# Attention values weighed in four column tiles of 32 instead of two of 64

## The chip, the cores and the metric

The kernel runs on one core of a Trainium2 chip. The metric is the device time of one execution in microseconds (us). The engines are named as the profile names them: PE is TensorE's matmuls and PEld its weight loads, DVE is VectorE, ACT is ScalarE, POOL is GpSimd, SP is SyncE.

## The reference, cut to what matters

64 graphs of 256 nodes with 512 features go through two layers of masked attention, each with a residual. All is float32.

```python
# layer 0: 4 heads of 64
h = relu(layernorm(x)); q, k, v = h @ Wq, h @ Wk, h @ Wv
sim = where(adj, einsum('bhid,bhjd->bhij', q, k) * 64**-0.5, -max)
x = x + einsum('bhij,bhjd->bhid', softmax(sim), v) @ Wo + bo
# layer 1: 8 heads of 64, the diagonal always allowed
h = relu(layernorm(x)); h = layernorm(h) * gamma + beta
q, k, v = split(h @ w_qkv.T, 3)
scores = where(adj | eye, einsum('bihd,bjhd->bhij', q, k) * 64**-0.5, -1e9)
x = x + einsum('bhij,bjhd->bihd', softmax(scores), v) @ w_out.T + b_out
```

The line that the change touches is the weighing of values, `softmax(sim) @ v`.

## The kernel before, in words

The kernel works in 32 steps of two graphs (`G` is 2, `g` counts them). Layer 0 of a step has 2 pairs of heads and layer 1 has 4, so a step has 6 units, a unit being one pair of heads (`pr`; `e` is the head in the pair) for both graphs: 192 units in all. Features or keys lie on the 128 partitions.

A unit goes through these functions:

- `scores` (L770): keys on partitions, queries along the free dimension. A head has 64 features, so the two heads use the two row halves of the array: 8 matmuls (2 graphs, 2 halves of the 256 keys, 2 heads) of 256 columns, into four PSUM tiles `sc`.
- `mask_scores` (L783, DVE) adds the mask, `exponentials` (L788, ACT) gives `p`, and `key_halves` (L792, POOL) adds the two key halves into `pd`.
- `weigh` (L802): the product of v and `p` over the 256 keys, into one PSUM tile `po` whose partitions are the 128 features of the pair. The weights that stay in the array are 128 keys by 64 features of v, so two heads stand side by side in the two column halves of the array. ACT copies `po` out (L816). Then come the sums over keys (L822): a block of 32 columns of ones times `pd`, four matmuls, one for each graph and head, in the four column quarters of the array. DVE takes reciprocals (L827) and their maximum (L828), and SP spreads them with eight DMAs.
- `normalise` (L843, POOL) multiplies by the reciprocals.

Around these stand the projections, as seven products of half-size blocks: `project_qk` (L679; L621, L625 and L627 are among its evacuations by DVE, and L689 is a multiplication on POOL that layer 0's q needs), `project_v0` (L706), `project_v1` (L720), the output products `combine0` (L731) and `combine1` (L745), and the transposes `transpose_h` (L600).

The order is written out by hand. Every call gets a due time in periods of 6.13 places (`at`, `at_dense`, `visit`), the calls are sorted by it, and each engine takes its instructions in that order; nothing reorders them afterwards. A `visit` puts one unit's `weigh` directly before the next unit's `scores`, so PE's stages follow as projection, weighing (L802), sums (L822), scores (L770), projection. PSUM is split into four tiles for scores and weighing (`ps_sc`) and four banks used in turn for all else (`mm_tile`).

Of the kernel before, what the change touches and what calls it, by code (L numbers as in the profile page):

```python
# [315 lines left out]
def fast_path(  # L316
# [20 lines left out]
    P = 128  # L337
    B, N, D = x.shape
    DH = 64
    G = 2  # L340
    NSTEP = B // G
    NIC = N // P
# [20 lines left out]
    def mm_tile(shape, dt=FP, hold=False):  # L363
        tag = next(b for b in banks if b not in held)
        banks.remove(tag)
        banks.append(tag)
        if hold:
            held.add(tag)
        return ps_mm.tile(shape, dt, name="mm", tag=tag)
# [424 lines left out]
    def weigh(s, lyr, pr, first):  # L794
        st = S[s]
        p, pd = st.pop(("p", lyr, pr))
        po = ps_sc.tile([P, G, N], FP, name="sc")
        for g in range(G):
            for kc in range(NIC):
                for e in range(2):  # L800
                    c0 = pr * P + e * DH
                    nc.tensor.matmul(  # L802
                        po[e * DH:(e + 1) * DH, g, :],
                        st[f"v{lyr}"][:, g * NIC + kc, c0:c0 + DH],
                        p[e][:, g, kc, :], start=(kc == 0), stop=(kc == NIC - 1),
                    )
        if lyr == 0:
            if first:
                st["oT0"] = act.tile([P, PR0, G, N], FP, name="oT0")
            dst = st["oT0"][:, pr]  # L810
        else:
            if first:
                st["oT1"] = act.tile([P, NB + 1, HP1, N], FP, name="oT1")
            b0, b1, step = B_OF[pr // HP1]
            dst = st["oT1"][:, b0:b1:step, pr % HP1, :]
        nc.scalar.copy(dst, po)  # L816

        sums = mm_tile([P, N])
        for g in range(G):
            for e in range(2):  # L820
                r0 = 32 * (2 * g + e)
                nc.tensor.matmul(  # L822
                    sums[r0:r0 + 32, :], ones, pd[:, e, g, :], start=True, stop=True
                )
        inv = sm.tile([P, N], FP, name="inv", bufs=1)
        for i in range(2):
            nc.vector.reciprocal(inv[:, i * P:(i + 1) * P], sums[:, i * P:(i + 1) * P])  # L827
        nc.vector.tensor_tensor_reduce(  # L828
            out=sums, in0=sums, in1=inv, scale=1.0, scalar=0.0, op0=ALU.add, op1=ALU.max,
            accum_out=extremes[:, units[0]:units[0] + 1],  # L830
        )
        units[0] += 1
        invb = sm.tile([P, G, N], FP, name="invb", bufs=1)
        for g in range(G):
            for e in range(2):
                r0 = 32 * (2 * g + e)
                for d0 in range(e * DH, (e + 1) * DH, 32):
                    nc.sync.dma_start(invb[d0:d0 + 32, g, :], inv[r0:r0 + 32, :])  # L838
        st["dst", lyr, pr] = dst, invb
# [29 lines left out]
    def visit(period, w, prev, cur):  # L869

        w -= 0.0003
        if 0 <= prev[0] < NSTEP:
            at(period, w, weigh, *prev)
            at(period, w + 0.55, normalise, *prev[:3])
        if 0 <= cur[0] < NSTEP:
            at(period, w, scores, *cur)
            at(period, w, mask_scores, *cur, 0)
            at(period, w + 0.05, exponentials, *cur, 0)
            at(period, w + 1 / 7, mask_scores, *cur, 1)
            at(period, w + 0.18, exponentials, *cur, 1)  # L880
            at(period, w + 0.2, key_halves, *cur, 0)
            at(period, w + 0.3, key_halves, *cur, 1)

    AT_C0, AT_Q0, AT_V0, AT_H1, AT_C1 = 3.0, 3.57, 4.57, 5.13, 5.131
    for s in range(-2, NSTEP):
        p = s
# [6 lines left out]
    for s in range(NSTEP):  # L893

        p = s - 2
# [14 lines left out]
        p = s - 1  # L910
# [13 lines left out]
        p = s  # L924
# [69 lines left out]
```

## Time and profile before

| what | value |
|---|---|
| time, median of 3 | 3520.03 us (3518.53 to 3522.54) |
| span of the profiled execution | 3519.7 us |
| PE busy | 3429.8 us, 97% |
| PEld, DVE, POOL, ACT busy | 75%, 57%, 54%, 35% |
| matmul records of the weighing, L802 | 3072 |
| matmul records of the sums over keys, L822 | 1536 |
| mean granted TensorE clock | 0.993 |

Busy time is a share of the span; an engine's idle time costs nothing unless another waits for it. A group such as `128*64 128x256 f32` is a matmul with 128 rows and 64 columns of the array in use, on a moving operand of 128 partitions by 256 float32. A float32 matmul leaves two records of matmul and two of weight load. The end of a matmul is modelled, so matmuls overlap in the record, and the distance between starts tells more than a duration.

### The profile page before, as it was taken

To read this page: it belongs to the slowest core of one execution; us is meant where nothing else is said; L and a number is where in the kernel's file an instruction comes from. 1 tells how busy PE (TensorE), PEld (TensorE's weight loads), DVE (VectorE), ACT (ScalarE), POOL (GpSimd) and SP (SyncE) were. 2 spreads that over 40 slices of the span, in tenths; PEclk is the share of its full clock that TensorE was granted. 3 is DMA by queue.
4 is the path that set the end of the run, shared out by engine and by line. 5 is a ranking of instruction groups with operands and counts; after the bars stand their busy time and mean duration, and the time that the engine had idled before them with its cause. 6 is when DMAs were issued, how large, how long until landed. Compare 5 with 4: busy or idle time off the path is not lost.

```text
span 3519.7 us, 52762 instructions
## 1 busy us (share of the span) xinstructions
PE 3429.8 (97%) x19555; PEld 2633.3 (75%) x19586; DVE 1988.8 (57%) x3681; ACT 1224.1 (35%) x2065; POOL 1905.5 (54%) x1643
## 2 busy tenths in 40 slices
PE   5999999999999999999999999999999999999997
PEld 3777777777777777777777777777777777777765
DVE  4465565555655555655655655556556556556553
ACT  2333333333333333333333333333333333333321
POOL 3556545556545565455565455665555654555642
PEclk9999999999999999999999999999999999999999
DMA  4011111110111111111111111101111111111011
GB/s 136 23 53 34 47 41 52 54 52 27 44 51 52 53 50 31 42 53 53 53 32 44 47 52 53 52 27 44 51 53 53 42 38 41 53 53 52 16 40 37
DMA packets 146968, 165.57 MB, mean 47 GB/s; under 512 B 43272, under 2 KB 94992, under 8 KB 146704
## 3 DMA queue, kind: packets, MB, share of 16 engines
q1 hardware_dynamic: 141312, 155.30, 14.8%
q10 hardware_dynamic: 5392, 6.82, 0.6%
q8 instruction: 157, 2.57, 0.3%
q14 instruction: 107, 0.88, 0.1%
HBM read 78.12 MB, written 33.55 MB: 32 GB/s over the span
## 4 chain that ended last, share of the span: by engine, by line
PE 88%; DVE 6%; POOL 2%; SPq 1%; DMA 1%; issue 1%; ACT 0%; ACTq 0%; POOLq 0%; DVEq 0%
PE mm L679 27%; PE mm L720 11%; PE mm L745 11%; PE sc L770 10%; PE sc L802 10%; PE mm L706 6%; PE mm L731 6%; PE mm L600 3%; PE mm L822 3%; SPq L838 1%; DVE bs L536 1%; DVE p L783 1%; POOL xt L493 1%; DVE ve L588 1%; DVE inv L827 1%
## 5 line engine op out<-in xcount | busy, mean ns | idle before, releaser
L792 POOL TENSOR_TENSOR pd<-p 128x512 f32<-128x512 f32 x384 | 485.8, 1280 | 1080.4 <-ACT p L788 1076.4
L679 PE MATMUL mm<-hT,wqkv 128*128 128x256 f32 x3584 | 802.0, 381 | 1.6
L679 PEld LDWEIGHTS mm<-hT,wqkv 128*128 128x128 f32 x3584 | 673.4, 190 | 111.4 <-issue 20.9
L788 ACT ACTIVATE p<-p 128x512 f32<-128x512 f32 x768 | 461.1, 629 | 509.9 <-DVE p L783 508.7
L827 DVE RECIPROCAL inv<-mm 128x128 f32<-128x128 f32 x384 | 339.5, 926 | 329.5 <-PE mm L822 309.0
L783 DVE TENSOR_TENSOR p<-sc,n 128x512 f32<-128x512 f32 x768 | 481.1, 682 | 2.2 <-PE sc L770 2.2
L816 ACT COPY oT<-sc 128x512 f32<-128x512 f32 x192 | 112.5, 586 | 1044.4 <-PE sc L802 1044.4
L679 PE MATMUL mm<-hT,wqk 128*128 128x256 f32 x1792 | 408.6, 383 | 11.9 <-DVE qk L621 11.8
L679 PEld LDWEIGHTS mm<-hT,wqk 128*128 128x128 f32 x1792 | 335.7, 190 | 90.7 <-DVE qk L621 23.8
L745 PE MATMUL mm<-wo,oT 128*128 128x256 f32 x1792 | 395.4, 381 | 5.9 <-POOL oT L843 5.9
L720 PE MATMUL mm<-wqkv,hT 128*128 128x256 f32 x1792 | 395.3, 381 | 0.0
L770 PE MATMUL sc<-qk 64*128 64x256 f32 x3072 | 386.6, 390 | 6.3 <-DVE qk L625 3.6
L802 PE MATMUL sc<-p,v 128*64 128x256 f32 x3072 | 379.4, 387 | 6.1 <-ACT p L788 6.1
L720 PEld LDWEIGHTS mm<-wqkv,hT 128*128 128x128 f32 x1792 | 337.8, 190 | 55.2 <-issue 10.6
L745 PEld LDWEIGHTS mm<-wo,oT 128*128 128x128 f32 x1792 | 339.7, 191 | 52.4 <-POOL oT L843 6.7
L770 PEld LDWEIGHTS sc<-qk 64*128 64x128 f32 x3072 | 280.1, 186 | 115.3 <-issue 65.8
L802 PEld LDWEIGHTS sc<-p,v 128*64 128x64 f32 x3072 | 205.9, 137 | 155.8 <-issue 61.9
L843 POOL TENSOR_TENSOR oT<-oT,invb 128x512 f32<-128x512 f32 x192 | 244.7, 1275 | 79.2 <-DMA invb<-inv 60.0
L648 POOL TENSOR_TENSOR xt<-xt,u 128x512 f32<-128x512 f32 x96 | 121.8, 1270 | 252.5 <-DVE xt L642 188.9
L550 ACT ACTIVATE h<-h,mr,r 128x512 f32<-128x512 f32 x256 | 203.3, 808 | 131.9 <-POOL mr L546 131.9
L638 DVE TENSOR_TENSOR xt<-mm,xt 128x512 f32<-128x512 f32 x64 | 44.3, 692 | 330.8 <-PE mm L745 330.8
L731 PE MATMUL mm<-wo,oT 128*128 128x512 f32 x512 | 230.6, 593 | 0.0
(104 smaller groups left out, 3821.4 us busy)
## 6 DMA issues: line engine op xcount, KB each, us to landing
invb<-inv SPq DMA_DIRECT2D x1536, 32.0 KB, 1.8
h<-in_x_dram SPq DMA_DIRECT2D x32, 1024.0 KB, 5.1
xt<-in_x_dram SPq DMA_DIRECT2D x32, 1024.0 KB, 5.1
out_dram<-xt SPq DMA_DIRECT2D x32, 1024.0 KB, 4.7
ad<-in_adj_dram SPq DMA_DIRECT2D x32, 128.0 KB, 4.4
wr<-in_L_gnn_w_qkv_dram ACTq DMA_DIRECT2D x3, 1024.0 KB, 10.3
wr<-in_L_gnn_w_out_dram ACTq DMA_DIRECT2D x1, 1024.0 KB, 14.4
wqk<-in_L_gnn_Wq_dram ACTq DMA_DIRECT2D x4, 128.0 KB, 5.1
```

The source lines that it names most:

```text
L679: nc.tensor.matmul(bank[:, k, :], w[:, wa, c, k, a * P:(a + 1) * P], st["hT"][:, ba, c, :], start=first and (k, c) == (0, 0), stop=(k, c) ...
L706: nc.tensor.matmul(bank, st["hT"][:, b0 + t // NIC * step, c % HC, i:i + P], wv0[:, c, :], start=(c == 0), stop=(c == NC - 1),)
L720: nc.tensor.matmul(bank[:, t, :], st["hT"][:, ba, c, t * P:(t + 1) * P], wqkv1[:, wa, c, 2, :], start=first and (t, c) == (0, 0), stop=(t, ...
L731: nc.tensor.matmul(bank, st["oT0"][:, pr, t // NIC, t % NIC * P:(t % NIC + 1) * P], wo0[:, pr, :], start=(pr == 0), stop=(pr == PR0 - 1),)
L745: nc.tensor.matmul(bank[:, t, :], st["oT1"][:, ba, c, t * P:(t + 1) * P], wo1[:, wa, c, :], start=first and (t, c) == (0, 0), stop=(t, c) ...
L770: nc.tensor.matmul(sc[g][e][:, kc, :], qk[rows, 1, k0:k0 + P], qk[rows, 0, g * N:(g + 1) * N], start=True, stop=True,)
L783: nc.vector.tensor_tensor(p[e][:, g], sc[e], neg[:, :, g, :], ALU.add)
L788: nc.scalar.activation(p[e][:, g], p[e][:, g], AF.Exp, scale=SCALE)
L792: nc.gpsimd.tensor_tensor(pd[:, e], p[e][:, :, 0, :], p[e][:, :, 1, :], ALU.add)
L802: nc.tensor.matmul(po[e * DH:(e + 1) * DH, g, :], st[f"v{lyr}"][:, g * NIC + kc, c0:c0 + DH], p[e][:, g, kc, :], start=(kc == 0), stop=(kc ...
L827: nc.vector.reciprocal(inv[:, i * P:(i + 1) * P], sums[:, i * P:(i + 1) * P])
L843: nc.gpsimd.tensor_tensor(dst, dst, invb, ALU.mult)
```

## The change

The weighing is cut finer: each head's 64 features of v become two blocks of 32, so that the array stands in four column tiles of 32, as it does for the sums over keys which follow. One head's two tiles read the same `p`. The purpose is that weighing and sums need no change of tiling between them. It is the only edit; the lines after it move up by one, so the weighing is L801 and the sums are L821 in the changed kernel.

```diff
         po = ps_sc.tile([P, G, N], FP, name="sc")
         for g in range(G):
             for kc in range(NIC):
-                for e in range(2):
-                    c0 = pr * P + e * DH
+                for r0 in range(0, P, 32):
                     nc.tensor.matmul(
-                        po[e * DH:(e + 1) * DH, g, :],
-                        st[f"v{lyr}"][:, g * NIC + kc, c0:c0 + DH],
-                        p[e][:, g, kc, :], start=(kc == 0), stop=(kc == NIC - 1),
+                        po[r0:r0 + 32, g, :],
+                        st[f"v{lyr}"][:, g * NIC + kc, pr * P + r0:pr * P + r0 + 32],
+                        p[r0 // DH][:, g, kc, :], start=(kc == 0), stop=(kc == NIC - 1),
                     )
```

The number of matmuls in a unit's weighing goes from 8 to 16, each with half the columns and the same 256 moving columns. Semaphores and the order of everything else are as before.

## The prediction

> **What bounds the kernel now.** I read the page's busy shares and its chain that ended last, then the costliest groups, then the chain and the timeline of one short stretch.
>
> ```profile
> span 3519.7 us, 52762 instructions
> PE 3429.8 (97%) x19555; PEld 2633.3 (75%) x19586; DVE 1988.8 (57%) x3681; ACT 1224.1 (35%) x2065; POOL 1905.5 (54%) x1643
> ...
> PE 88%; DVE 6%; POOL 2%; SPq 1%; DMA 1%; issue 1%; ACT 0%; ACTq 0%; POOLq 0%; DVEq 0%
> ...
> L802 PE MATMUL sc<-p,v 128*64 128x256 f32 x3072 | 379.4, 387 | 6.1 <-ACT p L788 6.1
> L802 PEld LDWEIGHTS sc<-p,v 128*64 128x64 f32 x3072 | 205.9, 137 | 155.8 <-issue 61.9
> ```
>
> TensorE is the bound: 97% busy, 88% of the chain, and its idle time before L802 is 6 us in all. What TensorE saves is saved by the kernel, unless some other engine stands right behind it. The changed matmuls are L802: 3072 records in 192 units (a unit is one head pair of one step), so 16 in a unit. A float32 matmul leaves two records, each with its own weight load: 8 matmuls, 16 records.
>
> A busy TensorE may still be waiting inside, because the ends of its matmuls are modelled. So I look at starts. The chain of waits in a steady stretch (start us, us, what):
>
> ```profile
> 1515.36 1.88 PE sc L802 x16
> 1517.24 0.57 PE mm L822 x8
> 1517.81 1.93 PE sc L770 x16
> 1519.73 12.28 PE mm L679 x56
> ```
>
> Full-array projections (L679) take 12.28/56 = 219 ns a record, 216 between neighbours (the rest is the seam at each end), the two-tile weighing 1.88/16 = 117 ns, the four-tile sums (L822) 0.57/8 = 71 ns. If tiles ran side by side at no cost these would be 216/2 = 108 and 216/4 = 54. The difference is a cost per stage, and the timeline of TensorE cut to a few ns at the seam shows where it sits:
>
> ```profile
> 1516.64 0.60 PE L802 MATMUL sc<-p,v 128*64 128x256 f32 x4
> ...
> 1516.85 0.39 PE L802 MATMUL sc<-p,v 128*64 128x256 f32 x2
> 1517.17 0.42 PE L822 MATMUL mm<-pd,ones 128*32 128x256 f32 x4
> ...
> 1517.41 0.40 PE L822 MATMUL mm<-pd,ones 128*32 128x256 f32 x4
> 1517.74 0.49 PE L770 MATMUL sc<-qk 64*128 64x256 f32 x2
> ```
>
> Read the first column. Inside the weighing, pairs start 0.21 apart (216 ns in the records' own starts). From its last pair to the first four of the sums it is 0.32 (316), from those four to the next four 0.24 (241), and from there to the scores 0.33 (326). The first step of a weighing is 267 ns, by the same starts. Steady steps are 216, so a seam between tilings costs 100 to 110 ns, and a stage that begins cold pays 51 ns with 64 weight columns, 25 with 32.
>
> **What the Trainium skill says.** "TensorEngine Tiling (Array Packing)", Key Properties: a change of tiling mode, not just of tile, drains the engine. The trace agrees: 100 ns where the tiling changes from L802 to L822, none where only buffer and product change inside the 56 records of L679. "TensorE: Matmul & The Clock Gate", LDWEIGHTS: a load takes its column count over 1.2 GHz, which as an estimate is 27 ns for 32 columns and 53 for 64; the trace's 25 and 51 at cold starts agree. The same page, The mechanism: tiles in different column groups run at once, started about 4 ns apart; in the records the four of L822 start 6 to 7 ns apart. No run here yet shows more than two fours in a row.
>
> **The change part by part.**
> Removed: 8 matmuls of 64 columns in a unit. Added: 16 of 32 columns. Streaming: a step moves 256 columns in 216 ns whatever the number of tiles side by side, by L679 (one tile), L802 (two) and the second four of L822. Before, 4 (graph, key half) x 2 passes = 8 steps of two tiles; after, 8 steps of four tiles. So 8 x 216 ns both times: nothing gained there.
> First step: 241 instead of 267, a load of 32 columns: 26 ns saved.
> Seam from weighing to sums: the same 128x32 tiling on both sides, so 216 instead of 316: 100 ns saved.
> First step of the sums: their weights can load behind the weighing's last four, so 216 instead of 241: 25 ns saved.
> Seams into the weighing (from full array) and out of the sums (to 64x128) stay. Sum: 26 + 100 + 25 = 151 ns a unit; weighing and sums take 2.295 us instead of 2.447.
> Twice as many instructions: 16 in 1.73 us, one per 108 ns. Waits of TensorE's queue for DMA at the start of the trace (24 to 28 us) have four float32 matmuls go by within 141 ns, 35 ns each, and at 71.9 us three matmuls of L822 that had stood behind a wait start 7 ns apart. So 108 ns is well within what the queue delivers: zero, hidden by the streaming. The waits are the same (for the exponentials and for the bank), standing on the same (graph, key half, head); both tiles of one head read the same p. DVE, ACT, POOL and SyncE keep their instruction lists and order; the copy L816 starts 0.12 us earlier after the weighing's start and hurries nobody.
>
> **Who stands right behind TensorE.** I looked for waits of TensorE that are met with less than 0.15 us to spare, stage by stage. Two recur once in a step. One is the projection after the fourth weighing of the step (L679 <- DVE qk L621, 30 times, 11.8 us in all); the chain back from it runs through DVE to a projection that comes after that unit's scores, so it moves with the gain and takes none. The other is in the timeline of the sixth unit:
>
> ```profile
> 1596.57 1.27 POOL L843 TENSOR_TENSOR oT<-oT,invb 128x512 f32<-128x512 f32 x1
> 1596.66 1.49 PEld L802 LDWEIGHTS sc<-p,v 128*64 128x64 f32 x16 [0.33 <-issue]
> 1597.81 1.27 POOL L689 TENSOR_TENSOR qk<-qk,ne 128x512 f32<-128x512 f32 x1
> 1599.12 1.38 PEld L770 LDWEIGHTS sc<-qk 64*128 64x128 f32 x14 [0.43 <-POOL qk L689]
> ```
>
> The scores there need qk, which POOL finishes at 1597.81 + 1.27 = 1599.08; they start at 1599.12. POOL is busy without a gap from 1594.09, where DVE's row statistics release it, all before this weighing begins at 1596.66. With the change the sums would let the scores go at 1596.66 + 2.295 = 1598.96: POOL isn't ready, and the scores still start at 1599.12. In that unit all is given back as a longer wait for POOL. The line of qk L689 lists 32 such waits of scores by TensorE's weight loads, 30 of them in steady steps.
>
> **Sum.** 192 units, of which 189 have the steady form (three at the start stand in long waits for inputs), less 30: 159 x 151 ns = 24.0 us. 3520.0 - 24.0 = 3496.0.
>
> **Rivals.**
> First: the wait for POOL doesn't take anything, because something shifts POOL's chain too. For: DVE, which releases it, is itself released by TensorE. Against: that release is before this weighing. All 192 units gain: 192 x 151 = 29.0, so 3491.0.
> Second: the gap at the seam is the end of any stage of small tiles, not of a change of tiling. For: it is 98 to 110 at every seam that the trace has, and each of these changes the tiling, so the trace can't part the two for small tiles. Against: full-array stages of different lines (L706 to L600 to L745) follow each other without one. Then only 26 + 25 = 51 ns a unit are saved: 159 x 51 = 8.1, so 3511.9.
> Third, the slower side: a run of fours doesn't reach 216. The trace has only one step from four to four, 241, and I take it for a cold load. If each step costs 241 because four loads can't be brought in behind four running tiles, weighing and sums take 9 x 241 + 326 = 2.495 us, 48 ns more than before: 192 x 48 = 9.3, so 3529.3. Against: loads of two tiles hide fully in L802's steady steps (next load 1 to 2 ns after its tile's matmul starts), and four of 32 columns are no more columns than two of 64.
>
> **How the numbers follow.** Forecast 0.70; first rival 0.10; second 0.10; third 0.10. The predicted time is the forecast's, 3496. The low end takes the first rival and a few us for run-to-run spread, 3488. The high end takes the second rival, or steps of 222 ns instead of 216 (10 x 6 = 60 ns a unit, 3505): 3512. The third rival, and part of the second, stay outside, about 1.5 in 10. The 0.2% bound is 7 us: the forecast and the first rival are faster, the second mostly (0.07), the rest same; third slower, with a bit to same. Faster 0.87, same 0.04, slower 0.09.
>
> **What would show it.** In the chain of the changed kernel: the weighing as x32 in about 1.75 us, the sums' x8 in about 0.54, no seam between them; starts of fours 216 apart. The scores' wait for POOL qk L689 grows from 0.43 to about 0.58 in 30 units, and the sum of that wait with it. Weight loads of 32 columns, 6144 of them. If fours start 240 apart, the third rival holds; if the seam stays at 0.31, the second; if the sixth unit is also 0.15 shorter, the first. I am wrong altogether if TensorE begins to wait for something that had room before.

## The result, and the profile after

| | before | after |
|---|---|---|
| time, median | 3519.85 us | 3499.25 us (3496.53 to 3501.51) |
| ratio, 95% interval | | 0.994 (0.9923 to 0.9957) |
| span of the profiled execution | 3519.7 us | 3496.7 us |

The changed kernel is faster by 0.6%: 20.6 us by the medians, 23.0 by the two profiled spans, where 24.0 were forecast. A second series beside later runs gave 3499.21 against 3520.82, ratio 0.9941 (0.9928 to 0.9955), and again a span of 3496.7.

The page of the changed kernel, the lines that answer to those of before:

```profile
span 3496.7 us, 58937 instructions
PE 3406.0 (97%) x22658; PEld 2627.7 (75%) x22658; DVE 1991.4 (57%) x3681; ACT 1224.0 (35%) x2065; POOL 1904.6 (54%) x1643
...
L801 PE MATMUL sc<-p,v 128*32 128x256 f32 x6144 | 376.7, 383 | 5.6 <-ACT p L788 5.6
L801 PEld LDWEIGHTS sc<-p,v 128*32 128x32 f32 x6144 | 181.7, 110 | 171.6 <-issue 61.7
```

The page barely shows what happened. TensorE is busy 97% as before, and the weighing's busy time goes from 379.4 to 376.7 us: its share of the gain seems to be 3 us. A group's busy time runs on to the modelled end of its last matmul, 379 ns after that one's start, and that covers the gap at a seam. The chain of waits in a steady stretch has it:

```profile
1508.01 1.86 PE sc L801 x32
1509.87 0.43 PE mm L821 x8
1510.30 1.93 PE sc L770 x16
1512.23 12.28 PE mm L679 x56
```

Weighing and sums took 1.88 + 0.57 = 2.45 us together and now take 1.86 + 0.43 = 2.29. The scores and the projection behind them are unchanged to 10 ns. (This view puts a boundary at the modelled end of the stage before, so it gives the saving to the sums; by starts, the weighing lasts 1.751 us instead of 1.878 and the sums 0.545 instead of 0.569.) TensorE's timeline, cut at the seam, has in the first column the starts of four records at a time (of two in the scores, the last line):

```profile
1509.47 0.40 PE L801 MATMUL sc<-p,v 128*32 128x256 f32 x4
1509.69 0.40 PE L821 MATMUL mm<-pd,ones 128*32 128x256 f32 x4
...
1509.90 0.40 PE L821 MATMUL mm<-pd,ones 128*32 128x256 f32 x4
1510.23 0.49 PE L770 MATMUL sc<-qk 64*128 64x256 f32 x2
```

From the weighing into the sums the step is now 0.22 (216 ns), from the sums to the scores it still is 0.33. Within the weighing the first step, from the first four records to the next, is 240 ns, and the six others are 216 each.

The sixth unit is the exception that was forecast. Its timeline on POOL and at TensorE's weight loads:

```profile
1588.49 1.29 POOL L842 TENSOR_TENSOR oT<-oT,invb 128x512 f32<-128x512 f32 x1
...
1589.73 1.28 POOL L689 TENSOR_TENSOR qk<-qk,ne 128x512 f32<-128x512 f32 x1
1590.12 0.35 PEld L821 LDWEIGHTS mm<-pd,ones 128*32 128x32 f32 x8
...
1591.07 0.95 PEld L770 LDWEIGHTS sc<-qk 64*128 64x128 f32 x10 [0.60 <-POOL qk L689]
```

The sums' loads are done at 1590.47, the scores' begin at 1591.07, when POOL has finished L689. The wait went from 0.43 to 0.60 us, where 0.58 was forecast. (Of these, 0.41 us is the idle time that the scores' loads have at this seam in other units too.) In the groups of all the scores' weight loads, first before and then after, the wait for POOL grew from 14.8 to 19.5 us; the growth of the wait for DVE qk L625 comes up at the end:

```profile
L770 PEld LDWEIGHTS sc<-qk 64*128 64x128 f32 x3072 | 280.1, 186 | 115.3 <-issue 65.8 <-POOL qk L689 14.8 <-DVE qk L625 7.5
L770 PEld LDWEIGHTS sc<-qk 64*128 64x128 f32 x3072 | 278.9, 186 | 122.7 <-issue 65.4 <-POOL qk L689 19.5 <-DVE qk L625 8.9
```

### The profile page after: what moved, and what is told of

Read it like the earlier page. It is cut to its first block, busy times and chain, and to the rows that moved or that the text cites. A ratio compares the mean times of both kernels' runs of the same rounds, so it can differ in the third digit from the quotient of the medians.

```text
span 3496.7 us, 58937 instructions
## 1 busy us (share of the span) xinstructions
PE 3406.0 (97%) x22658; PEld 2627.7 (75%) x22658; DVE 1991.4 (57%) x3681; ACT 1224.0 (35%) x2065; POOL 1904.6 (54%) x1643
## 4 chain that ended last, share of the span: by engine, by line
PE 83%; DVE 6%; POOL 5%; issue 3%; SPq 2%; DMA 1%; ACT 0%; POOLq 0%; ACTq 0%; DVEq 0%
PE mm L679 25%; PE mm L720 11%; PE mm L745 11%; PE sc L770 10%; PE sc L801 8%; PE mm L706 6%; PE mm L731 6%; PE mm L600 3%; PE mm L821 2%; SPq L837 2%; POOL oT L842 2%; POOL xt L493 1%; DVE bs L536 1%; DVE p L783 1%; POOL qk L689 1%
## 5 line engine op out<-in xcount | busy, mean ns | idle before, releaser
L679 PE MATMUL mm<-hT,wqkv 128*128 128x256 f32 x3584 | 802.0, 381 | 0.0
L679 PEld LDWEIGHTS mm<-hT,wqkv 128*128 128x128 f32 x3584 | 673.4, 190 | 111.4 <-issue 20.9
L679 PE MATMUL mm<-hT,wqk 128*128 128x256 f32 x1792 | 408.9, 383 | 11.8 <-DVE qk L621 11.8
L679 PEld LDWEIGHTS mm<-hT,wqk 128*128 128x128 f32 x1792 | 336.1, 190 | 90.4 <-DVE qk L621 23.8
L745 PE MATMUL mm<-wo,oT 128*128 128x256 f32 x1792 | 395.1, 381 | 5.8 <-POOL oT L842 5.8
L770 PE MATMUL sc<-qk 64*128 64x256 f32 x3072 | 388.1, 390 | 9.9 <-DVE qk L625 3.8
L801 PE MATMUL sc<-p,v 128*32 128x256 f32 x6144 | 376.7, 383 | 5.6 <-ACT p L788 5.6
L745 PEld LDWEIGHTS mm<-wo,oT 128*128 128x128 f32 x1792 | 339.1, 191 | 52.7 <-POOL oT L842 6.9
L770 PEld LDWEIGHTS sc<-qk 64*128 64x128 f32 x3072 | 278.9, 186 | 122.7 <-issue 65.4
L801 PEld LDWEIGHTS sc<-p,v 128*32 128x32 f32 x6144 | 181.7, 110 | 171.6 <-issue 61.7
```

The costliest lines, as they stand in the source:

```text
L679: nc.tensor.matmul(bank[:, k, :], w[:, wa, c, k, a * P:(a + 1) * P], st["hT"][:, ba, c, :], start=first and (k, c) == (0, 0), stop=(k, c) ...
L745: nc.tensor.matmul(bank[:, t, :], st["oT1"][:, ba, c, t * P:(t + 1) * P], wo1[:, wa, c, :], start=first and (t, c) == (0, 0), stop=(t, c) ...
L770: nc.tensor.matmul(sc[g][e][:, kc, :], qk[rows, 1, k0:k0 + P], qk[rows, 0, g * N:(g + 1) * N], start=True, stop=True,)
L801: nc.tensor.matmul(po[r0:r0 + 32, g, :], st[f"v{lyr}"][:, g * NIC + kc, pr * P + r0:pr * P + r0 + 32], p[r0 // DH][:, g, kc, :], start=(kc ...
```

## The experiments

All are compared by median, and by the span of the profiled execution; the ratios are to the kernel before. That kernel had 3521.58 us beside the first four and 3520.82 beside the last two.

**Is it the change of tiling, or any end of a stage of small tiles?** The trace of before couldn't part these. The changed kernel's 216 ns at the end of the weighing already speak for the tiling; the next two runs test it without any change to the weighing. One small matmul stands between weighing and sums, in the same tiling as both or in another. Its result lands in a corner of the sums' bank that the sums overwrite.

```diff
+        nc.tensor.matmul(sums[0:32, 0:32], ident[:, 0:32], ident[:, 0:32], start=True, stop=True)
```

> The changed kernel, and between the weighing and the sums of every unit one more matmul of 32 by 32 by 32, in the same tiling of 128x32 (into a corner of the sums' bank that the sums overwrite). Theory (the seam costs a drain when the tiling changes): no drain, only the small matmul's two passes of about 27 ns on one tile, so about 0.05 us a unit, 159 units: 8 us over the changed kernel, 3508; the step from the last four of the weighing to the small matmul is 216 ns. Rival (any end of a stage of small tiles costs about 100 ns): two ends more are there, the step is over 300 and the unit grows by 0.2 us or more, 3530 or above.

```diff
+        nc.tensor.matmul(sums[0:64, 0:32], ident[:, 0:64], ident[:, 0:32], start=True, stop=True)
```

> The same small matmul with 64 columns instead of 32, so in the tiling of 128x64: the tiling changes twice more in every unit. Theory: two drains (100 each), one cold load of 64 columns (51) and one of 32 (25) more than with 32 columns: about 0.27 us a unit over the run with 32 columns, 0.32 over the changed kernel; the units that wait for POOL hide 0.17 of it. 162 x 0.32 + 30 x 0.15 = 56 us over the changed kernel, 3555. Rival (end of stage, whatever the tiling): the same time as with 32 columns, within 5 us.

With 32 columns: 3506.35 us, span 3503.4, 6.7 over the changed kernel. With 64: 3560.09 us, span 3557.8, 61.1 over it, and slower than the kernel before (ratio 1.0109, 1.0094 to 1.0124). TensorE's timeline at the seam, first with 32 columns (the small matmul is L818, the sums are L822 in these two):

```profile
1512.51 0.40 PE L801 MATMUL sc<-p,v 128*32 128x256 f32 x4
1512.72 0.19 PE L818 MATMUL mm<-ident 128*32 128x32 f32 x1
1512.73 0.41 PE L822 MATMUL mm<-pd,ones 128*32 128x256 f32 x3
1512.75 0.20 PE L818 MATMUL mm<-ident 128*32 128x32 f32 x1
```

and with 64:

```profile
1508.85 0.40 PE L801 MATMUL sc<-p,v 128*32 128x256 f32 x4
1509.18 0.30 PE L818 MATMUL mm<-ident 128*64 128x32 f32 x2
1509.41 0.40 PE L822 MATMUL mm<-pd,ones 128*32 128x256 f32 x1
```

In the same tiling the small matmul follows after 0.21 (216 ns), and three sums on the other tiles have started before its second pass. A unit grows by 43 ns. With 64 columns it follows after 0.33, the sums after another 0.23, and the sums' first step is 240 again: a unit grows by 369 ns (113 + 232 + 24). The small matmul with another number of columns costs more than eight times as much, so the gap belongs to the change of tiling. The second rival of the prediction falls. The forecasts were 3508 and 3555; the second was 5 us low, mainly because a unit had been put at 0.32 us.

**Does POOL take the sixth unit's gain?** That unit's weighing alone is put back to two tiles:

```diff
+        w = DH if (lyr, pr) == (1, 3) else 32
...
-                for r0 in range(0, P, 32):
+                for r0 in range(0, P, w):
...
```

The lines left out put `w` for 32 in the two slices.

> The changed kernel with the sixth unit's weighing (layer 1, last pair) back in two tiles of 64; the other five stay at four of 32. Theory (the sixth unit's gain is given back as a wait of the scores for POOL qk L689): the same time as the changed kernel within 1 us in the span of the profile, and that wait falls from 19.5 us to about 15. Rival (the wait takes nothing, the whole gain counts): 30 x 0.15 = 4.5 us slower than the changed kernel, 3504.

3499.84 us (3497.16 to 3500.17), span 3496.8 against 3496.7. By starts, the sixth unit's weighings take 1.878 us again and the others 1.751 (but for a few that wait at the start), with no effect on the span. What the weighing loses, the wait of the scores gets back; the line of qk L689 in that kernel, among those who waited for it (us, times):

```profile
  PEld sc L770: 14.6, 32
```

It is 19.5 in the changed kernel, and about 15 was forecast. From the other side, POOL is relieved ahead of that multiplication:

```diff
-            at(p, 4.35 + 0.1 * t, second_bias, s, t)
+            at(p, 4.6 + 0.1 * t, second_bias, s, t)
```

> The changed kernel with the four adds of the second bias on POOL put 0.25 of a period later, so that one add of 1.27 us no longer stands before the sixth unit's q multiplication (L689). Theory: that multiplication ends about 1.2 us earlier, the scores no longer wait for it, and the sums of the sixth unit take 0.545 us like the others instead of 0.72: 30 x 0.176 = 5.3 us less than the changed kernel, 3494. Rival (POOL isn't what holds that unit): no change beyond 1 us.

3495.44 us (3494.87 to 3495.56), ratio 0.9927 (0.9913 to 0.994), span 3493.4. The same line of qk L689 in that kernel:

```profile
  PEld sc L770: 1.7, 2
```

The steady waits are gone, and the two left are at the start. All 189 sums before scores together take 104.2 us instead of 109.6: 5.4 less, where 5.3 were expected. The span fell by 3.3 only. One projection at the start (L745 to L679, once in a run) took 13.4 us instead of 12.2; it took 13.5 in the run before and 12.4 in the kernel before, so this lies in the variation of the start and is no effect of the edit that I can name.

The same edit on the kernel before, as the control:

> The kernel before with the second bias on POOL put 0.25 of a period later, the same edit as in the run of the changed kernel with that name. Theory: before the change the scores of the sixth unit waited only 16 ns for POOL qk L689, so 30 x 0.016 = 0.5 us at most: the same time as before within 1 us. Rival (the later bias helps by itself, whatever the tiling): 3 to 5 us faster than before, as it was on the changed kernel.

3520.4 us against 3520.82, ratio 0.9999 (0.9991 to 1.0007). The later bias is worth next to nothing before the change: the sums fell by 0.7 us in all. (The 16 ns of the expectation are one unit's; the median of the 30 is 23.) POOL was the last to be ready there before, but by so little that moving it gained next to nothing; the faster TensorE made a wait of about 0.18 us of it.

**The other wait that the prediction found.** After the fifth weighing of a step in PE's order, L679 waits for DVE qk L621, 30 times, before and after alike. (That weighing is layer 1's second pair, which prediction and expectation call the fourth; it is the fourth if the pairs are counted by number.) DVE does row statistics ahead of L621; here the last of them goes behind it, on top of the later bias:

```diff
-            at(p, (3.55, 3.7, 4.05, 4.2)[t], norm1_rest, s, t)
+            at(p, (3.55, 3.7, 4.05, 4.3)[t], norm1_rest, s, t)
```

> The changed kernel with the later second bias, and with the last of layer 1's row statistics put behind DVE qk L621 in the fourth unit, so that the projection there no longer waits for it. The 40 records of L679 in that place take 9.49 us where 40 x 0.216 and two seams would be 8.83: 0.66 us in 30 steps. If nothing else stands behind TensorE: 30 x 0.66 = 20 us under the changed kernel with the later bias, 3476. If POOL's row scale L545, which then starts later against TensorE, holds up the q multiplication L689 again, as I work out by about 0.2 us: 3482.

3479.6 us, ratio 0.9883 (0.9868 to 0.9898), span 3477.3: the fastest kernel here, 1.2% under the kernel before. The stage of 40 records takes 8.83 us instead of 9.49, as worked out, and the wait for L621 is off the list of TensorE's waits. The wait for POOL is back; the line of qk L689 once more:

```profile
  PEld sc L770: 20.5, 32
```

0.66 us x 30 = 19.8 are taken out and 5.9 given back at the sums of the sixth unit (all 189 sums take 110.1 us instead of 104.2): net 13.9, and the span fell by 16.1. The forecast for this case was 3482. Of the 2.2 us more, 1.3 lie in the projection at the start, 12.1 us here, and 0.7 before TensorE's first matmul and after its last.

## Why the prediction was right, point by point

- Streaming: 8 steps of 216 ns whether two or four tiles run side by side. Right. This was the step with the least behind it: the trace of before had one step from four to four, 240 ns, and the second four of L822, which the prediction names for 216, has a seam behind it (329). The 240 was a cold load, as taken; the third rival (241 each time; its sum is 9.2 us, not 9.3) falls with the seven steps of 216 that follow the first of every weighing, the last of them into the sums.
- First step with 32 columns instead of 64: 26 ns; measured 267 to 240, 27.
- Seam between weighing and sums: 100 ns; measured 316 to 216, 100. That it is the change of tiling is shown by the pair with the small matmul. Over all units of the trace of before, the four kinds of seam cost 93 to 113 ns over a steady step, a little wider than the 98 to 110 of the prediction.
- First step of the sums: 25 ns; measured 240 to 216, 24.
- A unit: 151 ns forecast, 2.447 to 2.296 measured, 151.
- Twice as many instructions at no cost: right, since after its first step no steady weighing has a step longer than 216.
- The sixth unit: no gain forecast; by starts, its weighing and sums took 2.470 us before and 2.474 after (medians of 30). The first rival (it gains too) falls by the two experiments on POOL.
- The wait of L679 for DVE L621 moves with the gain and takes none: right, it is 11.8 us before and after.
- The sum: 24.0 forecast, 23.0 between the profiled spans, 20.6 and 21.6 by the medians of the two series, with 4 to 5 us between the lowest and the highest of each kernel. By starts, all weighings and sums together fell by 23.7 us, so this part of the forecast is right. The scores, L770, grew by 1.2.
- Most of that 1.2 is a third place where TensorE has little to spare, and the prediction's list of two lacks it. The scores behind the fourth weighing of a step, in PE's order, need, for their second graph, what DVE writes in L625. DVE comes to L625 only after work on the masks (L525, L528) that waited for POOL L522. In the changed kernel:

```profile
1028.71 1.29 DVE L525 SCALAR_TENSOR_TENSOR n<-mm,n 128x512 bf16<-128x512 f32 x2 [4.58 <-POOL n L522]
1029.92 0.68 DVE L528 TENSOR_SCALAR ne<-mm 128x512 f32<-128x512 f32 x1
1030.51 0.68 DVE L625 TENSOR_TENSOR qk<-mm,qk 128x512 f32<-128x512 f32 x1
...
1031.25 0.73 PEld L770 LDWEIGHTS sc<-qk 64*128 64x128 f32 x8 [1.00 <-DVE qk L625]
```

In the two profiles of kernels with all units in two tiles, 11 and 10 of 30 such stages are held by more than 5 ns, by 6.1 and 5.6 us in all. In the five in which the weighing has four tiles (in one of them all but the sixth unit's) and nothing stands between it and the sums, it is 21 to 23 stages and 6.8 to 9.2 us; with the small matmul in between, which makes the units slower again, 11 and 6 stages, 6.7 and 3.8 us. So the faster TensorE is held there more often and some of the gain is given back, about 1 us in the pair compared here. The size differs by 2 us between two profiles of the same changed kernel, no run tests this wait by an edit, and why POOL is late in some steps and not in others stays open.

## What to carry to other kernels

Look at the starts at the seams between stages of TensorE, not at its busy share: a change of tiling costs here about as much as half a step of streaming (100 of 216 ns), and neighbours that share a tiling save it, even at twice the number of matmuls. Then ask for each place how long the next producer has been ready: where it was ready only just in time, the gain ends up there as a wait, and an edit worth nothing before can be worth taking after.

## What I had not expected

Tiles of one tiling run on without waiting for each other even across stages. With the small matmul on the first tile, the sums on the three other tiles started 7 to 20 ns after it and before its second pass, no later than without it; only the first tile's sums started 60 ns later. The second passes of the other three then came 23 ns later, those of the first 63.

The weighing's group in the page fell by 2.7 us, TensorE's busy time as a whole by 23.8 (3429.8 to 3406.0). The last matmul of a weighing is taken to end 379 ns after its start; the sums started 0.31 us after it before and 0.20 now, so the two groups overlap by more than before, which the whole counts once and the groups twice. Neither names a seam; only the starts do.
